# Mamba-2 block and ternary FFN on one core: the scan of sequence 0 issued beside the input projection of sequence 1, with changed start-up order

## Chip, cores and metric

One Trainium2 chip, one of its cores. The metric is the device time of one execution in microseconds; the number that is compared is the median of several executions.

## What is computed

Sixteen sequences of 512 tokens, 256 features each. Float32 throughout, apart from the ternary matmul passes. Cut to what matters, for one x:

```python
x1 = layernorm(x)
zxbcdt = x1 @ in_proj_w.T                    # 256 -> 512 (z) + 768 (xBC) + 8 (dt)
xBC = silu(causal_conv4(xBC) + conv_b)       # -> xs (512), B (128), C (128)
dt = softplus(dt + dt_bias); dA = exp(dt * -exp(A_log))
# for every token, 8 heads of 64 channels, state of 128:
S = dA * S + (xs * dt) outer B;   y = S @ C + D * xs
y = y * silu(z);  y = y * rsqrt(mean(y*y) + 1e-5) * norm_w
x = x + layernorm(x1 + y @ out_proj_w.T)
h = gelu(layernorm(x) @ ternary(W1).T + b1)
x = x + layernorm(h @ ternary(W2).T + b2)
# ternary(w): round(w / mean(|w|)) clipped to -1, 0, 1
```

## The kernel before, in words

The kernel keeps all weights in SBUF and works through the 16 sequences. The order of instructions on PE, ACT, DVE and POOL is written out by hand: every stage is a Python generator that issues instructions and yields a weight of work, and `interleave` (L812) takes, again and again, the next step of the stream that is least far through its window. A stream is given as (generator, work, from, to), with the window as shares of the whole. `run` issues one stage without anything beside it. SP's queue, which carries nearly all DMAs, follows the order of issue.

The stages of one sequence:

- `stage_a0` (L417): statistics of the layernorm on DVE (`bn_stats`, L254), its power on POOL (L261), and four ACT instructions that normalise x to x1 (L285).
- `stage_t0` (L429): PE transposes x1 in eight pieces (L303), ACT copies the two halves to x1T (L306).
- `stage_a` (L312): the input projection in blocks, in the order of a string. "b" is one of six blocks of xBC: four matmuls pm (L325), ACT scales them to cv (L330), DVE adds three convolution taps (L332), and ACT's silu (L339) is held back in a list `late` until the next block. "z" is one of four blocks of z with its silu (L347, L351). "d" makes the rows of dt (L359, L364), "t" turns them over by a PE transpose (L369) and starts the softplus on DVE (L370 to L377). The six blocks and the four of z take PSUM tiles from one pool of four buffers, `ps_a`, which the scan uses too.
- `stage_a1` (L407): the silu that the softplus needs. `stage_a2` (L437): the softplus in 16 small DVE instructions (L444 to L462), then the sums of dt*A over tokens by three kinds of small matmuls (L474, L475), with copies on DVE (L477 to L486) and ACT (L480), and three DMAs that carry the split sums through HBM into the operands lhs_e and rhs_e of the decay matmuls (L488 to L492).
- `stage_b0` and `stage_d` (L499, L514): exponentials of the sums on ACT (L504, L509), written to HBM and broadcast to all partitions as ct (1.5 MB, L519). `stage_e` (L525): POOL multiplies ct by C in three instructions (L530).
- `stage_b1` (L537): for each of four chunks of 128 tokens two decay matmuls pe (L546) and their exponentials mt on ACT (L550).
- `stage_b2` (L555): the scan over the four chunks. `prepare` transposes the inputs (px, L590), makes xdt (L592), the products of B and C (pg, L596 to L603), xend on POOL (L605) and the masked mt (L608) on DVE. Then come pst (L625), the state (L628, L630, L633), the outputs py (L641, L648), y on DVE (L654), the gate zs on POOL (L658), and squares (L569 to L571).
- `stage_c1` and `stage_c2` (L672, L745): output projection, the second layernorm and the feed-forward part, one sequence behind.

Constants for the decay matmuls are made on POOL and ACT by `exponent_constants` (L122). `scales` (L208) folds norm_w into w_out on ACT (L210) and finds the mean of |W| of both ternary weights: a DVE reduction (L215), a matmul with ones (L218), three small DVE instructions (L220 to L223), four POOL comparisons (L227). `ternary` (L231) then makes the ternary weights on DVE.

The start of the kernel, up to sequence 2, is in this order: stage_a of sequence 0 with the constants and the layernorm of sequence 1; stage_a of sequence 1 with stage_a2 of sequence 0 and `scales`; then the scan of sequence 0 with stage_a2 of sequence 1, `ternary(1)` and the layernorm of sequence 2. From sequence 1 on, the scan of a sequence stands beside the feed-forward part of the one before it.

Of the kernel before, what the change touches and what calls it, by code (L numbers as in the profile page):

```python
# [29 lines left out]
F32 = mybir.dt.float32  # L30
# [27 lines left out]
def mamba_ffn_kernel(  # L58
# [96 lines left out]
    nc.scalar.dma_start(cw_sb, conv_w)  # L155
    cb_sb = const.tile([P, NCV], F32)
    nc.scalar.dma_start(cb_sb, conv_b)
    nc.sync.dma_start(win_sb[:, :, 0:DI], win_v[:, :, 0:DI])
    wdt_sb = const.tile([P, 2, 32], F32)
    nc.gpsimd.memset(wdt_sb, 0.0)  # L160
    nc.sync.dma_start(wdt_sb[:, :, 0:NH], win_v[:, :, DI + CONV :])

    dtb = const.tile([P, 1], F32)
    nc.gpsimd.memset(dtb, 0.0)
    for b in range(1, min(3, NB)):
        load_x(b)
# [22 lines left out]
    w1_bf = const.tile([P, 2, FF], BF16)  # L189
    w2_sb = const.tile([P, NF, DM], F32)  # L190
    nc.sync.dma_start(w2_sb, w2.rearrange("(k p) n -> p k n", p=P))
    for c in range(NC):
        nc.sync.dma_start(dtb[32 * c : 32 * c + NH, :], dt_bias.rearrange("(h o) -> h o", o=1))

    negA = const.tile([P, NH], F32)
    nc.scalar.activation(negA, alog, AF.Exp)
# [11 lines left out]
    def scales():  # L208
        for k in range(DI // P):
            nc.scalar.activation(  # L210
                wo_sb[:, k, :], wo_sb[:, k, :], AF.Copy, scale=nw_sb[:, k : k + 1]
            )
        for n, (w, low, _) in ternaries.items():
            part = small.tile([P, 1], F32, tag="tpart", name=f"tpart_{n}")
            nc.vector.tensor_reduce(part, w, AX.XY, ALU.add, apply_absolute_value=True)  # L215
            yield 2.0
            tot = ps_tr.tile([P, 512], F32, tag="tr", name=f"ttot_{n}")
            nc.tensor.matmul(tot[:, 0:1], ones, part, start=True, stop=True)  # L218
# [5 lines left out]
            flat = w.rearrange("p k n -> p (k n)")  # L224
# [84 lines left out]
        return t.rearrange("p (h d) -> p h d", h=NH)  # L309


    def stage_a(b, kinds):  # L312
        x1, x1T = normed.pop(b)


# [6 lines left out]
        def block(m):  # L322
            pm = ps_a.tile([P, L], F32, tag="a", name=f"pm_{b}_{m}")
            for k in range(2):
                nc.tensor.matmul(  # L325
                    pm, win_sb[:, k, DI + m * P : DI + (m + 1) * P], x1T[:, k, :],
                    start=(k == 0), stop=(k == 1),
                )
            cv = sb.tile([P, L], F32, tag="cv", name=f"cv_{b}_{m}", bufs=3)
            nc.scalar.activation(cv, pm, AF.Copy, scale=cw_sb[:, m, 3:4])  # L330
            for j in range(1, 4):
                nc.vector.scalar_tensor_tensor(  # L332
                    cv[:, j:], pm[:, 0 : L - j], cw_sb[:, m, 3 - j : 4 - j], cv[:, j:],
                    ALU.mult, ALU.add,
                )
# [17 lines left out]
        def dt_rows():  # L353


            pq = ps_a.tile([P, L], F32, tag="a", name=f"pq_{b}")
            for k in range(2):
                for c in range(NC):
                    nc.tensor.matmul(  # L359
                        pq[32 * c : 32 * (c + 1), 0:P], wdt_sb[:, k, :],  # L360
                        x1T[:, k, c * P : (c + 1) * P], start=(k == 0), stop=(k == 1),
                    )
            rows = small.tile([P, P], F32, tag="dtr", name=f"dtr_{b}", bufs=1)
            nc.scalar.activation(rows, pq[:, 0:P], AF.Identity, bias=dtb)  # L364
            return rows

        def dt_turned(rows):
            pq = ps_a.tile([P, L], F32, tag="a", name=f"pqt_{b}")
            nc.tensor.transpose(pq[:, 0:P], rows, ident)  # L369
            nc.vector.tensor_copy(  # L370
                dt, pq[:, 0:P].rearrange("p (c h) -> p c h", c=NC)[:, :, 0:NH]
            )

            neg = small.tile([P, NC * NH], F32, tag="sp_n", name=f"sp_n_{b}")
# [31 lines left out]

    def stage_a1(b):  # L407

        s = seqs[b]
        while s["late"]:  # L410
            s["late"].pop()()
        s["sil"] = small.tile([P, NC * NH], F32, tag="sp_s", name=f"sp_s_{b}")
        nc.scalar.activation(s["sil"], s["neg"], AF.Silu)
        yield 0.1

# [51 lines left out]
    def sums_of(b, a):  # L467
# [8 lines left out]
        sums = small.tile([P, 2, W], F32, tag="sums", name=f"sums_{b}")  # L476
        nc.vector.tensor_copy(sums.rearrange("p i w -> p (i w)"), pd[:, 0 : 2 * W])  # L477
        pc = pd[0:W, 2 * W : 2 * W + P]
        cum = small.tile([W, P], F32, tag="dtr", name=f"cum_{b}", bufs=1)
        nc.scalar.copy(cum, pc)  # L480
        cp = small.tile([W, 3, P], BF16, tag="cp", name=f"cp_{b}", bufs=1)
        rest = small.tile([W, P], F32, tag="cr", name=f"cr_{b}", bufs=1)
# [72 lines left out]
    def stage_b2(b):  # L555
        s = seqs[b]
        dt, xbc, zs, dec, mts = s["dt"], s["xbc"], s["zs"], s["dec"], s["mts"]
        ct = s.pop("ct")

        def over_d(t):  # L560
            return t.unsqueeze(2).to_broadcast([P, NH, HD])
# [246 lines left out]
    def chain(*stages):  # L808
        for st in stages:
            yield from st  # L810
# [35 lines left out]
    def run(stage):  # L846
        for _ in stage:
            pass

    with tc.manual_schedule(engines=ordered):  # L850
# [17 lines left out]
        run(stage_a1(1))  # L868
        run(stage_b0(0))
        run(stage_d(0))  # L870
        for i in range(NB - 1):
            if i > 0:
                interleave(
                    (ending(), 0.1, 0.0, 0.01),
                    *([(ternary(2), 4.0, 0.1, 0.7)] if i == 1 else []),
                    *([(stage_a6(i), 0.1, 0.02, 0.03)] if i > 1 else []),
                    (stage_a(i + 1, BESIDE), A_WORK - 1.72, 0.0, 1.0),
                    (stage_c1(i - 1), C1_WORK, 0.0, 1.0),
                    (stage_e(i), E_WORK, 0.06, 1.0),
                )  # L880
                run(stage_a1(i + 1))
# [6 lines left out]
            if i > 0:  # L888
                second.append((stage_c2(i - 1), C2_WORK, 0.02, 1.0))
                second.append((stage_b2(i), B2_WORK, 0.0, 0.98))  # L890
                second.append((stage_a2(i + 1), A2_WORK, 0.15, 0.5))
                second.append((stage_a5(i + 1), 1.7, 0.58, 0.66))
            else:
                second.append((stage_b1(0, 0, NC), 4 * B1_WORK, 0.0, 0.1))
                second.append((stage_e(0), E_WORK, 0.0, 0.3))
                second.append((stage_b2(0), B2_WORK, 0.04, 0.98))
                second.append((stage_a2(1), A2_WORK, 0.03, 0.5))
                second.append((ternary(1), 4.0, 0.3, 0.7))
# [58 lines left out]
```

## Time and profile before

| what | value |
|---|---|
| median of 3 executions | 1191.05 us (1191.03 to 1191.07) |
| profiled execution, its own time | 1192.11 us |
| its span | 1190.4 us |
| busy: PE, DVE, POOL, ACT | 93%, 72%, 50%, 47% |
| PE busy from 0 to 122.73 us | 78.40 us, granted clock 0.83 |
| DVE, ACT, POOL busy from 0 to 122.73 us | 73.04, 49.60, 45.64 us |

The span is what the profile covers; the execution's time lies 1.7 us above it. PE is the matmul engine, PEld its weight loads, DVE, ACT and POOL are VectorE, ScalarE and GpSimd; a `q` behind a name is that engine's DMA issuing. The granted clock is the share of full speed that TensorE had. A name such as pm or xdt is the tile that an instruction writes, and L325 is a line of the kernel. An instruction that waits holds up everything behind it on its own engine.

### The profile page before, as it was taken

To read this page: it belongs to the slowest core of one execution; us is meant where nothing else is said; L and a number is where in the kernel's file an instruction comes from. 1 tells how busy PE (TensorE), PEld (TensorE's weight loads), DVE (VectorE), ACT (ScalarE), POOL (GpSimd) and SP (SyncE) were. 2 spreads that over 40 slices of the span, in tenths; PEclk is the share of its full clock that TensorE was granted. 3 is DMA by queue.
4 is the path that set the end of the run, shared out by engine and by line. 5 is a ranking of instruction groups with operands and counts; after the bars stand their busy time and mean duration, and the time that the engine had idled before them with its cause. 6 is when DMAs were issued, how large, how long until landed. Compare 5 with 4: busy or idle time off the path is not lost.

```text
span 1190.4 us, 16908 instructions
## 1 busy us (share of the span) xinstructions
PE 1112.2 (93%) x6104; PEld 731.1 (61%) x6164; DVE 851.5 (72%) x2213; ACT 564.1 (47%) x951; POOL 595.6 (50%) x707
## 2 busy tenths in 40 slices
PE   6746989999999999999999999999999999998697
PEld 2324557575766757576665757566575757666475
DVE  4766786868777686868768686877768687775552
ACT  4531554645454464546356454635546463542321
POOL 2156545545454555546355454635455454545732
PEclk9877999999999999999999999999999999999899
DMA  5010101010110102011020201002020101101000
GB/s 191 2 55 10 65 4 72 18 66 27 36 57 4 71 19 75 19 57 36 4 74 17 73 19 66 27 4 89 4 71 19 66 27 32 44 4 71 2 9 26
DMA packets 28547, 48.57 MB, mean 41 GB/s; under 512 B 6576, under 2 KB 25648, under 8 KB 26416
## 3 DMA queue, kind: packets, MB, share of 16 engines
q1 hardware_dynamic: 27056, 47.33, 11.7%
q8 instruction: 48, 0.79, 0.3%
q10 hardware_dynamic: 1408, 0.16, 0.1%
q14 instruction: 35, 0.29, 0.1%
HBM read 38.44 MB, written 9.04 MB: 40 GB/s over the span
## 4 chain that ended last, share of the span: by engine, by line
PE 83%; POOL 7%; DVE 6%; ACT 3%; issue 1%; DMA 0%; POOLq 0%; ACTq 0%; DVEq 0%
PE pf L787 19%; PE pm L325 14%; PE ph L753 11%; PE po L707 9%; PE pz L347 8%; PE py L641 5%; PE pst L625 4%; PE py L648 3%; POOL x3p L741 3%; PE pe L546 2%; DVE cv L332 2%; POOL xend L605 1%; PE pt_a L303 1%; PE px L590 1%; PE pss L577 1%; PE pt_f L733 1%
## 5 line engine op out<-in xcount | busy, mean ns | idle before, releaser
L332 DVE SCALAR_TENSOR_TENSOR cv<-pm,cw_sb,cv 128x511 f32<-128x511 f32 (+2 forms) x288 | 215.3, 748 | 54.1 <-ACT cv L330 46.2
L787 PE MATMUL pf<-w_sb,hT 128*128 128x256 f32 x1024 | 248.8, 383 | 0.0
L787 PEld LDWEIGHTS pf<-w_sb,hT 128*128 128x128 f32 x1024 | 189.9, 190 | 42.3 <-issue 14.3
L325 PE MATMUL pm<-x1T,win_sb 128*128 128x512 f32 x384 | 187.9, 614 | 5.1 <-ACT x1T L306 5.1
L753 PE MATMUL ph<-x3p,w_bf 128*128 128x512 bf16 x723 | 181.0, 379 | 6.3 <-ACT x3p L740 1.8
L658 POOL TENSOR_TENSOR zs<-y,zs 128x512 f32<-128x512 f32 x64 | 82.4, 1288 | 203.6 <-DVE y L654 203.6
L759 ACT ACTIVATE hT<-ph,b_sb 128x512 f32<-128x512 f32 x128 | 87.9, 688 | 127.9 <-PE ph L753 91.4
L753 PEld LDWEIGHTS <-w_bf 128*128 128x128 bf16 x768 | 72.7, 98 | 93.3 <-issue 28.3
L550 ACT ACTIVATE mt<-pe 128x512 f32<-128x512 f32 x128 | 74.1, 597 | 116.2 <-PE pe L546 114.1
L707 PE MATMUL po<-wo_sb,zs 128*128 128x256 f32 x512 | 124.3, 387 | 0.3 <-DVE att L713 0.3
L330 ACT ACTIVATE cv<-pm,cw_sb 128x512 f32<-128x512 f32 x96 | 65.7, 684 | 123.8 <-PE pm L325 122.2
L347 PE MATMUL pz<-x1T,win_sb 128*128 128x512 f32 x256 | 121.9, 599 | 0.0
L325 PEld LDWEIGHTS pm<-x1T,win_sb 128*128 128x128 f32 x384 | 72.5, 196 | 78.8 <-issue 67.7
L530 POOL TENSOR_TENSOR ct<-ct,xbc 128x1024 f32<-128x1024 f32 x48 | 113.4, 2375 | 12.5 <-DVE sp_a L456 12.5
L707 PEld LDWEIGHTS po<-wo_sb,zs 128*128 128x128 f32 x512 | 95.7, 192 | 28.5 <-issue 17.1
L654 DVE SCALAR_TENSOR_TENSOR y<-xbc,dsk,py 128x128 f32<-128x128 f32 x256 | 71.2, 340 | 44.0 <-PE py L648 23.5
L641 PE MATMUL py<-mt,xdt 128*64 128x128 f32 x1024 | 99.2, 289 | 2.7 <-DVE y L654 2.3
L793 DVE TENSOR_TENSOR o<-pf,b_sb 128x256 f32<-128x256 f32 x64 | 26.9, 420 | 88.1 <-PE pf L787 88.1
L641 PEld LDWEIGHTS py<-mt,xdt 128*64 128x64 f32 x1024 | 62.9, 143 | 32.9 <-issue 18.6
L347 PEld LDWEIGHTS pz<-x1T,win_sb 128*128 128x128 f32 x256 | 47.9, 193 | 56.1 <-issue 48.2
L351 ACT ACTIVATE zs<-pz 128x512 f32<-128x512 f32 x64 | 37.9, 592 | 87.5 <-PE pz L347 87.3
L648 PE MATMUL py<-ct,state 128*64 128x128 f32 x768 | 78.2, 283 | 0.0
(137 smaller groups left out, 1805.3 us busy)
## 6 DMA issues: line engine op xcount, KB each, us to landing
ct<-way SPq DMA_DIRECT2D x16, 1536.0 KB
xin<-in_x SPq DMA_DIRECT2D x16, 512.0 KB
out<-o SPq DMA_DIRECT2D x30, 256.0 KB
w_in<-in_w SPq DMA_DIRECT2D x1, 1024.0 KB
w_sb<-in_w SPq DMA_DIRECT2D x1, 1024.0 KB, 11.0
win_sb<-in_w_in SPq DMA_DIRECT2D x1, 768.0 KB
win_sb<-in_w_in SPq DMA_DIRECT2D x1, 512.0 KB
wo_sb<-in_w_out SPq DMA_DIRECT2D x1, 512.0 KB
```

Of the source, the lines that this page charges most:

```text
L325: nc.tensor.matmul(pm, win_sb[:, k, DI + m * P : DI + (m + 1) * P], x1T[:, k, :], start=(k == 0), stop=(k == 1),)
L332: nc.vector.scalar_tensor_tensor(cv[:, j:], pm[:, 0 : L - j], cw_sb[:, m, 3 - j : 4 - j], cv[:, j:], ALU.mult, ALU.add,)
L347: nc.tensor.matmul(pz, win_sb[:, k, j * P : (j + 1) * P], x1T[:, k, :], start=(k == 0), stop=(k == 1),)
L530: nc.gpsimd.tensor_tensor(ct[:, c - 1], ct[:, c - 1], xbc[:, 5, c * P : (c + 1) * P].unsqueeze(1).to_broadcast([P, NH, P]), ALU.mult,)
L550: nc.scalar.activation(mt[:, hs, :].rearrange("p h t -> p (h t)"), pe, AF.Exp)
L641: nc.tensor.matmul(py[h % 2 * HD : (h % 2 + 1) * HD, j, :], xdt[:, h * HD : (h + 1) * HD], mts[c][:, h, :], start=True, stop=(c == 0),)
L648: nc.tensor.matmul(py[h % 2 * HD : (h % 2 + 1) * HD, j, :], state[:, h * HD : (h + 1) * HD], ct[:, c - 1, h, :], start=False, stop=True,)
L658: nc.gpsimd.tensor_tensor(zs[:, :, tok], y, zs[:, :, tok], ALU.mult)
L707: nc.tensor.matmul(po[:, 0:DM], g[:, k, c * P : (c + 1) * P], wo_sb[:, k, :], start=(k == 0), stop=(k == NJ - 1),)
L753: nc.tensor.matmul(ph, w1_bf[:, k, f * P : (f + 1) * P], x3p[:, j, k, :], start=(j == 0 and k == 0), stop=(j == 2 and k == 1),)
L759: nc.scalar.activation(hT[:, f, :], ph, AF.Gelu, bias=b1_sb[:, f : f + 1])
L787: nc.tensor.matmul(pf[:, 0:DM], hT[:, f, c * P : (c + 1) * P], w2_sb[:, f, :], start=(f == 0), stop=(f == NF - 1),)
```

## The change

Ten small edits, all in the start-up. The input of sequence 1 is loaded ahead of z's weights. dt_bias is broadcast over partitions by one DMA on ACT's queue, in place of four on SP's, and is added by DVE after the transpose of dt, in place of ACT before it. The sums of |W| are made by ACT (Abs with an accumulator) in place of DVE. `stage_a` gets a lag for its held silus, two blocks for sequence 0. `stage_sil` is split from `stage_a1`. The tile `cum` gets a buffer of its own. The strings of blocks for sequences 0 and 1 put dt second. The statistics of sequence 1 are issued ahead of sequence 0's convolutions, and softplus and sums of sequence 0, and `scales`, in its `stage_a`. The scan of sequence 0 is interleaved with `stage_a` of sequence 1, together with its own softplus, the decay matmuls of sequence 1, the layernorm of sequence 2 and `ternary(1)`. In POOL's order xend of chunks 0 and 1 comes ahead of the first product on ct.

```diff
-    nc.sync.dma_start(win_sb[:, :, 0:DI], win_v[:, :, 0:DI])
     wdt_sb = const.tile([P, 2, 32], F32)
     nc.gpsimd.memset(wdt_sb, 0.0)
     nc.sync.dma_start(wdt_sb[:, :, 0:NH], win_v[:, :, DI + CONV :])
-
-    dtb = const.tile([P, 1], F32)
-    nc.gpsimd.memset(dtb, 0.0)
-    for b in range(1, min(3, NB)):
-        load_x(b)
+    load_x(1)
+    nc.sync.dma_start(win_sb[:, :, 0:DI], win_v[:, :, 0:DI])
+    load_x(2)
+    dtb = const.tile([P, NH], F32)
+    nc.scalar.dma_start(dtb, dt_bias.partition_broadcast(P))
...
-    for c in range(NC):
-        nc.sync.dma_start(dtb[32 * c : 32 * c + NH, :], dt_bias.rearrange("(h o) -> h o", o=1))
...
-            nc.vector.tensor_reduce(part, w, AX.XY, ALU.add, apply_absolute_value=True)
+            flat = w.rearrange("p k n -> p (k n)")
+            nc.scalar.activation(low, flat, AF.Abs, accum_out=part)
...
-    def stage_a(b, kinds):
+    def stage_a(b, kinds, lag=1):
...
-            while late:
-                late.pop()()
             late.append(
...
+            if len(late) > lag:
+                late.pop(0)()
...
-            nc.scalar.activation(rows, pq[:, 0:P], AF.Identity, bias=dtb)
+            nc.scalar.copy(rows, pq[:, 0:P])
...
-            nc.vector.tensor_copy(
-                dt, pq[:, 0:P].rearrange("p (c h) -> p c h", c=NC)[:, :, 0:NH]
-            )
+            nc.vector.tensor_tensor(
+                dt, pq[:, 0:P].rearrange("p (c h) -> p c h", c=NC)[:, :, 0:NH],
+                dtb.unsqueeze(1).to_broadcast([P, NC, NH]), ALU.add,
+            )
...
     def stage_a1(b):
 
+        late = seqs[b]["late"]
+        while late:
+            late.pop()()
+        yield from stage_sil(b)
+
+    def stage_sil(b):
...
-        cum = small.tile([W, P], F32, tag="dtr", name=f"cum_{b}", bufs=1)
+        cum = small.tile([W, P], F32, tag="cum", name=f"cum_{b}", bufs=1)
...
-    EVEN, BESIDE = "bzbdzbtzbzbb", "bbdtzbzbzbz"
+    FIRST, SECOND, BESIDE = "bdbtbzbzbzbz", "bdbtzbzbzbzb", "bbdtzbzbzbz"
...
         interleave(
             (
-                chain(stage_a0(0), stage_t0(0), stage_a(0, EVEN)),
+                chain(stage_a0(0), stage_t0(0), stage_a(0, FIRST, 2)),
                 A0_WORK + T0_WORK + A_WORK, 0.0, 1.0,
             ),
-            (exponent_constants(), 9.0, 0.15, 0.9),
-            (stage_a0(1), A0_WORK, 0.4, 0.9),
+            (exponent_constants(), 9.0, 0.1, 0.5),
+            (stage_a0(1), A0_WORK, 0.04, 0.28),
+            (chain(stage_sil(0), stage_a2(0)), 0.1 + A2_WORK, 0.42, 0.85),
+            (scales(), 6.0, 0.55, 1.0),
         )
         run(stage_t0(1))
-        run(stage_a1(0))
+        run(stage_a6(0))
         interleave(
-            (stage_a2(0), A2_WORK, 0.0, 0.6),
-            (scales(), 6.0, 0.35, 0.9),
-            (stage_a(1, EVEN), A_WORK, 0.0, 1.0),
+            (stage_a(1, SECOND), A_WORK, 0.0, 0.8),
+            (stage_b0(0), 0.1, 0.11, 0.111),
+            (stage_d(0), 0.1, 0.111, 0.112),
+            (stage_b1(0, 0, NC), 4 * B1_WORK, 0.112, 0.1121),
+            (stage_b2(0), B2_WORK, 0.2, 0.9),
+            (stage_e(0), E_WORK, 0.3, 0.65),
+            (chain(stage_sil(1), stage_a2(1)), 0.1 + A2_WORK, 0.3, 0.75),
+            (stage_a0(2), A0_WORK, 0.6, 0.85),
+            (ternary(1), 4.0, 0.75, 0.95),
+            (stage_a6(1), 0.1, 0.86, 0.861),
+            (stage_b0(1), 0.1, 0.88, 0.881),
+            (stage_b1(1, 0, 2), 2 * B1_WORK, 0.89, 0.9),
+            (stage_b1(1, 2, 4), 2 * B1_WORK, 0.94, 0.98),
+            (stage_d(1), 0.1, 0.95, 0.96),
+            (stage_t0(2), T0_WORK, 0.96, 1.0),
         )
-        run(stage_a1(1))
-        run(stage_b0(0))
-        run(stage_d(0))
-        for i in range(NB - 1):
-            if i > 0:
+        for i in range(1, NB - 1):
...
             second.append((stage_c2(i - 1), C2_WORK, 0.02, 1.0))
             second.append((stage_b2(i), B2_WORK, 0.0, 0.98))
...
```

More of the change, by code (lines that the diff above doesn't have):

```diff
@@ L223, in scales @@
             nc.vector.tensor_scalar_mul(nhalf, half, -1.0)
-            flat = w.rearrange("p k n -> p (k n)")
             for j in range(4):
@@ L369, in dt_turned @@
             nc.tensor.transpose(pq[:, 0:P], rows, ident)
-            nc.vector.tensor_copy(
-                dt, pq[:, 0:P].rearrange("p (c h) -> p c h", c=NC)[:, :, 0:NH]
+            nc.vector.tensor_tensor(
+                dt, pq[:, 0:P].rearrange("p (c h) -> p c h", c=NC)[:, :, 0:NH],
+                dtb.unsqueeze(1).to_broadcast([P, NC, NH]), ALU.add,
             )
-            neg = small.tile([P, NC * NH], F32, tag="sp_n", name=f"sp_n_{b}")
+            neg = small.tile([P, NC * NH], F32, tag="sp_n", name=f"sp_n_{b}", bufs=2)
             df = dt.rearrange("p c h -> p (c h)")
@@ L407, in stage_a1 @@
     def stage_a1(b):
+        late = seqs[b]["late"]
[3 more added lines that the diff above has]
+    def stage_sil(b):
         s = seqs[b]
-        while s["late"]:
-            s["late"].pop()()
-        s["sil"] = small.tile([P, NC * NH], F32, tag="sp_s", name=f"sp_s_{b}")
+        s["sil"] = small.tile([P, NC * NH], F32, tag="sp_s", name=f"sp_s_{b}", bufs=1)
         nc.scalar.activation(s["sil"], s["neg"], AF.Silu)
@@ L557, in stage_b2 @@
         dt, xbc, zs, dec, mts = s["dt"], s["xbc"], s["zs"], s["dec"], s["mts"]
-        ct = s.pop("ct")
+        ct = s["ct"]
         def over_d(t):
@@ L860, in mamba_ffn_kernel @@
+            (scales(), 6.0, 0.55, 1.0),
         )
         run(stage_t0(1))
-        run(stage_a1(0))
+        run(stage_a6(0))
         interleave(
-            (stage_a2(0), A2_WORK, 0.0, 0.6),
-            (scales(), 6.0, 0.35, 0.9),
-            (stage_a(1, EVEN), A_WORK, 0.0, 1.0),
-        )
-        run(stage_a1(1))
-        run(stage_b0(0))
-        run(stage_d(0))
-        for i in range(NB - 1):
-            if i > 0:
[L873 to L879, printed above, removed]
-                )
-                run(stage_a1(i + 1))
+            (stage_a(1, SECOND), A_WORK, 0.0, 0.8),
[13 more added lines that the diff above has]
+            (stage_t0(2), T0_WORK, 0.96, 1.0),
+        )
@@ L882, in mamba_ffn_kernel @@
+        for i in range(1, NB - 1):
+            interleave(
+                (ending(), 0.1, 0.0, 0.01),
+                *([(ternary(2), 4.0, 0.1, 0.7)] if i == 1 else []),
+                *([(stage_a6(i), 0.1, 0.02, 0.03)] if i > 1 else []),
+                (stage_a(i + 1, BESIDE), A_WORK - 1.72, 0.0, 1.0),
+                (stage_c1(i - 1), C1_WORK, 0.0, 1.0),
+                (stage_e(i), E_WORK, 0.06, 1.0),
+            )
+            run(stage_a1(i + 1))
             second = [
@@ L887, in mamba_ffn_kernel @@
             ]
[L888 to L898, printed above, removed]
+            second.append((stage_c2(i - 1), C2_WORK, 0.02, 1.0))
+            second.append((stage_b2(i), B2_WORK, 0.0, 0.98))
+            second.append((stage_a2(i + 1), A2_WORK, 0.15, 0.5))
+            second.append((stage_a5(i + 1), 1.7, 0.58, 0.66))
             second.append((stage_d(i + 1), 0.1, 0.92, 0.93))
```

## Prediction

> **What bounds the kernel now.** I read the page first: PE is busy 93% of the span, so the steady part has little to give, and its slices fall only at the two ends. Then busy time by stretch, cut where the first convolution matmul of sequences 1 (39.20) and 2 (122.73) starts. Columns: length, then busy time of PE, PEld, DVE, ACT, POOL, granted clock, DMA share, GB/s.
>
> ```profile
> 39.20:122.73 83.53, 54.42 (x248) 30.29 (x250) 54.62 (x120) 28.67 (x57) 35.65 (x28) 0.76 0.12 40
> 122.73:190.00 67.27, 63.36 (x354) 40.55 (x357) 54.21 (x132) 31.50 (x54) 32.80 (x37) 1.00 0.08 24
> 190.00:257.00 67.00, 66.25 (x376) 43.52 (x379) 51.52 (x136) 33.57 (x57) 35.11 (x42) 1.00 0.10 33
> ```
>
> From 192.95 on a sequence takes 68.5 us (x1T copies at 192.95, 261.45, 329.95; the first such step, from 121.40, takes 71.55), and PE is busy 66.25 of 67.00 at clock 1.00. There the kernel is bound by PE and the change leaves its work and order alone. Ahead of that PE idles 83.53 - 54.42 = 29.1 us, and at clock 0.76 about 0.24 x 54.4 = 13.1 us of its busy time is clock: 42 us in one stretch. No engine there exceeds 65%; it is bound by waits. So the forecast is one difference: when does sequence 2's first matmul start, 122.73 now. What it gains goes through one to one, because PE has no slack behind it.
>
> The waits of the first 122.7 us (total, times, longest):
>
> ```profile
> DVE cv L332 <- ACT cv L330: 21.4, 8, 9.1
> ...
> ACT cum L480 <- DVE sums L477: 11.1, 2, 8.6
> ...
> PE pst L625 <- DVE sp_a L456: 6.7, 1, 6.7
> ...
> PE pm L325 <- ACT x1T L306: 5.1, 1, 5.1
> PE ttot L218 <- DVE tpart L215: 4.9, 1, 4.9
> ...
> PE pe L546 <- DMA rhs_e<-away: 3.9, 1, 3.9
> ```
>
> DVE waits for convolutions while PE waits for the scan's inputs, one after the other: the scan of sequence 0 has no matmul-rich neighbour. Last, rows in order of time (start, duration) that price operations:
>
> ```profile
> 46.86 0.87 DVE L456 SCALAR_TENSOR_TENSOR sp_a<-sp_a,sp_e 128x32 f32<-128x32 f32 x4
> ...
> 50.95 2.28 DVE L215 TENSOR_REDUCE tpart<-w_in 128x1 f32<-128x2048 f32 x1
> ...
> 73.26 0.21 ACT L413 ACTIVATE sp_s<-sp_n 128x32 f32<-128x32 f32 x1
> 73.49 1.28 ACT L504 ACT_TABLE_LOAD   x1
> ...
> 74.78 0.26 ACT L504 ACTIVATE dec<-sums 128x64 f32<-128x64 f32 x1
> ...
> 82.64 3.82 DVE L456 SCALAR_TENSOR_TENSOR sp_a<-sp_a,sp_e 128x32 f32<-128x32 f32 x4
> 83.07 2.34 POOL L530 TENSOR_TENSOR ct<-ct,xbc 128x1024 f32<-128x1024 f32 x1 [12.52 <-DVE sp_a L456]
> ```
>
> The same four DVE instructions take 0.87 alone and 3.82 beside POOL's ct product. Convolution taps (one operand from PSUM) keep their 0.75 beside POOL.
>
> **Part 1, up to sequence 1's first matmul (39.20 now).** The start to 16.5 stays: pm of block 0 ends there at half clock. Moved onto the SP queue ahead of z's weights is load_x(1). SP's third issue waits for a small ACT-queue load until 7.55, as now, so x_1 takes the slot of z's weights; the 4 MB behind move at 340 to 400 GB/s from 11 on, so x_1 lands near 12.5, z's weights near 14 (needed at 21), wdt near 16. wdt is needed at 16.5 instead of 20.3; I charge nothing, up to 1.5 if it is late. The dt_bias broadcast is one more ACT-queue DMA and replaces four tiny SP issues (4.7 us of SP, after which dt_rows waited 2.2 now); DVE adds the bias in the instruction that copied: 0.2 either way.
>
> Sequence 1's statistics take DVE 4 x 0.53 + 0.35 = 2.5 us, 12.5 to 15, ahead of the first taps, which can't start before 17.3: covered. The queue behind it on DVE is all taps; cover gone means 1:1. POOL's power and product (1.2) follow, and all rhs_e/lhs_e constants (6.3) now stand behind them, done near 22.7 instead of 31.6; ACT's copies want them at 24: covered. ACT puts the four x_1 (2.07) ahead of cv 1, so cv 1 comes at 20.5 instead of near 19: 1 us on DVE.
>
> Following the ACT and DVE orders with row durations (cv 0.69, silu 0.71, zs 0.59, rhs_e copy 1.03, taps 2.32): cv 2 ends 21.8, table load 23.1, silu, copies and softplus silu to 27.7, cv 3 28.4, silu, w_out scaling 1.69, absolute sum, zs 1, cv 4 at 34.0. PE, done with pm 4 at 28, stands at ttot for the absolute sum until 32.7: 4.8 us idle, half clock behind it. DVE does taps 3 to 30.7, twelve softplus steps (0.19 each) to 33.0, taps 4 to 36.3, thalf, sums. ACT's cum, behind silu 2, waits for these sums to 37.0 (2.3; the same row has 2.5 now), then zs 2, absolute sum, cv 5 at 40.7; taps 5 end at 43.0, thalf 43.5. PE's transposes of x_1 stand behind the second ttot and share its two PSUM buffers, so they wait for that thalf; with the x1T copies, sequence 1's matmul starts near 45.4. That is 6.2 later, with sequence 0's softplus, sums and both scales already done.
>
> Absolute sums: DVE loses 2 x 2.28. On ACT no such row exists; two of the 1024-wide copies give 2 x 1.03, less one fixed part: 1.9 to 2.1. The Trainium skill ("ScalarE: Activation LUTs", Rules for kernel authors) says simple arithmetic belongs on VectorE, per element up to about three times faster. By that rule 2.28 on DVE would become some 6.8; by the rows 1.9. I take the rows: the DVE price is a measured float32 reduction, and the rule's factor is for bf16. The accumulator may add 0 to 0.3 each.
>
> **Part 2, to sequence 2's first matmul (83.5 now).** PE does pm 0, pq, pm 1 by 50.3 (first at half clock); ACT cv 0, dt, cv 1, silu 0, then the exp table at 51.7, dec, cum, eight mt (0.5 each) from 53.6 to 57.7. Their inputs by DMA: cp at 38.5, landing 4 us later, so the 3.9 wait for rhs_e goes. The pe matmuls take turns through PSUM with mt; pqt, queued behind them, comes at 56.5, and DVE, whose next instruction it feeds, idles 53.3 to 56.6. What is late next is this: 3.3 us that did not exist.
>
> Chunk 0 prepares on DVE 59.0 to 61.5 (xdt 0.69, two small 0.6, mt 1.21), chunk 1 to 64.0. xend now stands ahead of ct on POOL: today xend of chunk 0, ready at 80.2, ran at 85.4 behind ct, which waited for its 1.5 MB broadcast; pst now runs at 62.0. The broadcast, issued 55.2, needs 6.4 (76.7 to 83.1 now): 61.6, no wait. Then DVE is the chain: taps 2 to 66.3, y0 1.1, four softplus steps, chunk 2 2.5, four steps, state, taps 3 to 76.6, y1 to 77.7, eight steps, chunk 3 2.5, taps 4, state to 87.5, half the statistics, sums, y2 to 91.4, rest, taps 5 from 92.9 to 95.2. Pure DVE work from 48.7 to 95.2 is 36.3 (taps 13.9, chunks 9.4, y 3.4, softplus and dt 4.1, states 1.4, statistics 2.8, sums 1.3); 3.3 is the pqt idle; the rest, 6.9, is short waits and contention.
>
> Contention is the unknown. Sixteen softplus steps fall beside POOL's ct, zs, state. Ends: 0 if none collides; 16 x 2.1 = 34 if each waits as the worst row (L462: 2.27 for 0.19). I take 5.5, near today's 2.95 + 0.97 + 2.08 = 6.0 of the same steps of sequence 1. PE waits for a at 82: 4.4 idle, half clock for a few us, hidden by DVE.
>
> The tail: silu 5 at 96.4 (behind the four x_2), exp table 98.4, dec, cum 98.9, seven mt 102.4, x1T; matmul of sequence 2 near 103.5. w_bf (2.6) hides beside mt. I add 2.5 for some 25 handovers at 0.1 that I rounded away: **106**.
>
> Tables: the exp/silu alternation adds two loads. The skill (same page, Table sets: the hidden batching unit) says to do all of one set before switching, and prices a switch at about 2.66 with its drain: 5.3. The rows show silu ending 73.47, load 1.28, exp at 74.78: no drain seen, 2.6. One more lies on my chain than now; it is in the walk at 1.28. By the rule it would be 1.4 later.
>
> Sum: 122.73 - 106 = 16.7, rounded to 16. The profiled execution took 1192.11 with span 1190.4 and gives 1176.1 and 1174.4; the median of 3, 1191.05, is 1.06 below it, so **1175.0**.
>
> **Rivals.** (a) Waits vanish more than I think: DVE from 48.7 with 36.3 of work and no idle ends at 85, tail 8.3, so 93 to 96 and a gain of 27 to 29: 1163. For it: PE gets matmul cover, clock 1.00. Against: pqt and POOL. Chance 0.10.
>
> (b) The early statistics and absolute sums stretch part 1: wdt late 1.5, cold clock, ttot; 8 us more than walked: 1183. Chance 0.20.
>
> (c) Slower: the second softplus now runs amid POOL's scan products. At 2.1 for each of 16 steps, 34 instead of 5.5 on the DVE chain, sequence 2 starts at 134.5, 12 later: 1203. It decides from 5.5 + 16.7 = 22 us of contention on (1.4 a step). For it the row 3.82; against it, ten of the sixteen steps today kept 0.2. Chance 0.09.
>
> (d) The new order shifts waits only, within 2.4 us: 1191. Chance 0.03. My forecast: 0.58.
>
> A measurement can tell about 0.2%, 2.4 us, from no change. Range 1166 to 1188: the forecast +-9 and most of (b); left out are (a), (c), (d). Faster 0.88, same 0.03, slower 0.09.
>
> **What would show it.** After: the first matmul of sequence 2 near 106, sequence 1 near 45; clock in between above 0.9; no pst wait behind ct; two more ACT_TABLE_LOAD at 1.28; ACTIVATE of 128x2048 near 1.9; DVE's wait at dt for pqt near 3; 71.6 and then 68.5 us per sequence behind. Wrong if the softplus steps of sequence 1 together exceed 12 us, if x_1's statistics hold the first taps, or if the steady stretch changes.

## The result and the profile after

The changed kernel takes 1174.79 us in the median of 4 runs (1172.91 to 1177.73), the kernel before 1191.04 on the same chip (4 runs, 1190.73 to 1191.07): ratio 0.9869, 95% interval 0.9855 to 0.9883. The forecast was 1175.0. The profiled execution took 1172.91 us with a span of 1171.1, which is 19.2 us less than the profiled execution of before. Line numbers from here on are those of the changed kernel: pm is L323, cv L328, the taps L330, the softplus L447 to L465, the sums pd L477, ct L533, pe L549, mt L553, px L593, xdt L595, xend L608.

Sequence 1's first matmul starts at 42.05 us (39.20 before) and sequence 2's at 102.90 (122.73 before). The busy times by stretch, cut at these two points, in the same columns as before (length; PE, PEld, DVE, ACT, POOL; granted clock, DMA share, GB/s):

```profile
42.05:102.90 60.85, 45.43 (x241) 24.51 (x240) 47.12 (x94) 29.53 (x54) 29.30 (x25) 0.82 0.11 37
102.90:170.00 67.10, 64.06 (x351) 40.83 (x351) 53.54 (x129) 30.55 (x52) 31.76 (x36) 0.96 0.10 34
170.00:237.00 67.00, 66.46 (x380) 43.52 (x379) 51.86 (x137) 33.72 (x57) 34.13 (x42) 1.00 0.10 33
```

The stretch is 60.85 us in place of 83.53, and it starts 2.85 later: 22.68 - 2.85 = 19.8 us are won at the start of sequence 2. Behind it the x1T copies come at 102.15, 173.96, 242.45 and 310.95: one step of 71.8 and then 68.5, against 71.55 and 68.5 before. So 0.3 us of the 19.8 is given back in the first step, and nearly all of the rest arrives at the end (the span is 19.3 shorter). The stretch is denser but not full: PE idles 60.85 - 45.43 = 15.4 us (29.1 before), and its clock is 0.82.

The waits of the first 103 us (total, times, longest) show what took the place of the old ones:

```profile
ACT cum L483 <- DVE sums L480: 14.9, 2, 12.5
...
PE pd L477 <- DVE a L465: 8.4, 2, 8.1
DVE cv L330 <- ACT cv L328: 8.2, 7, 2.9
...
PE ttot L216 <- ACT w_in L213: 3.9, 1, 3.9
DVE xdt L595 <- PE px L593: 3.9, 1, 3.9
```

DVE's wait for convolutions falls from 21.4 to 8.2. PE's waits for pst (6.7) and pm (5.1) are gone, and the one for rhs_e falls from 3.9 to 1.6. In their place PE waits 8.1 us for the softplus of sequence 1 (row "PE pd"), and DVE waits for pqt, PE's transpose of dt (3.0), and then for px (3.9). In order of time:

```profile
52.62 0.19 DVE L368 TENSOR_TENSOR dt<-pqt,dtb 128x32 f32<-128x32 f32 x1 [2.98 <-PE pqt L367]
52.86 3.77 PE L345 MATMUL pz<-x1T,win_sb 128*128 128x512 f32 x4 [0.28 <-DVE dt L368]
57.11 0.69 DVE L595 TENSOR_TENSOR xdt<-px,dt 128x512 f32<-128x512 f32 x1 [3.86 <-PE px L593]
```

ACT's rows of the same execution, in order of time, price the two operations on which the prediction weighed a rule:

```profile
29.61 1.90 ACT L213 ACTIVATE w_in<-w_in 128x2048 f32<-128x2048 f32 x1
31.41 0.19 ACT L213 ACTIVATION_READ_ACCUMULATOR w_in<-w_in 128x1 f32 x1
...
96.45 0.70 ACT L335 ACTIVATE xbc<-cv,cb_sb 128x512 f32<-128x512 f32 x1
97.16 1.28 ACT L507 ACT_TABLE_LOAD   x1
98.45 0.26 ACT L507 ACTIVATE dec<-sums 128x64 f32<-128x64 f32 x1
```

The absolute sum is 1.90 plus a separate instruction of 0.19 that reads the accumulator. The table switch is 1.28, with the last silu ending 0.01 ahead of it and dec starting 0.01 behind: no drain.

### The profile page after: what moved, and what is told of

It reads as the page before. It is cut to its first block, busy times and chain, and to the rows that moved or that the text cites. A ratio compares the mean times of both kernels' runs of the same rounds, so it can differ in the third digit from the quotient of the medians.

```text
span 1171.1 us, 16958 instructions
## 1 busy us (share of the span) xinstructions
PE 1110.8 (95%) x6164; PEld 727.9 (62%) x6164; DVE 849.0 (72%) x2211; ACT 568.0 (48%) x957; POOL 593.7 (51%) x706
## 4 chain that ended last, share of the span: by engine, by line
PE 83%; DVE 6%; POOL 6%; ACT 3%; DMA 1%; issue 1%; POOLq 0%; ACTq 0%; DVEq 0%
PE pf L790 20%; PE pm L323 12%; PE ph L756 12%; PE po L710 9%; PE pz L345 8%; PE py L644 5%; PE pst L628 4%; PE py L651 3%; POOL x3p L744 3%; PE pe L549 2%; DVE cv L330 1%; POOL xend L608 1%; PE pt_a L300 1%; PE px L593 1%; PE pt_f L736 1%
## 5 line engine op out<-in xcount | busy, mean ns | idle before, releaser
L330 DVE SCALAR_TENSOR_TENSOR cv<-pm,cw_sb,cv 128x511 f32<-128x511 f32 (+2 forms) x288 | 215.3, 747 | 44.8 <-ACT cv L328 36.9
L756 PE MATMUL ph<-x3p,w_bf 128*128 128x512 bf16 x768 | 189.0, 381 | 4.2 <-ACT x3p L743 1.7
L323 PE MATMUL pm<-x1T,win_sb 128*128 128x512 f32 x384 | 184.1, 602 | 0.0
L756 PEld LDWEIGHTS <-w_bf 128*128 128x128 bf16 x768 | 72.9, 98 | 93.8 <-issue 29.1
L553 ACT ACTIVATE mt<-pe 128x512 f32<-128x512 f32 x128 | 73.6, 595 | 110.3 <-PE pe L549 110.3
L328 ACT ACTIVATE cv<-pm,cw_sb 128x512 f32<-128x512 f32 x96 | 65.7, 684 | 118.7 <-PE pm L323 117.1
L323 PEld LDWEIGHTS pm<-x1T,win_sb 128*128 128x128 f32 x384 | 70.9, 193 | 71.8 <-issue 65.7
L533 POOL TENSOR_TENSOR ct<-ct,xbc 128x1024 f32<-128x1024 f32 x48 | 113.3, 2374 | 0.0
L611 DVE SCALAR_TENSOR_TENSOR mt<-mt,pg 128x1024 f32<-128x1024 f32 x64 | 77.6, 1212 | 0.5
```

The source lines that it names most:

```text
L323: nc.tensor.matmul(pm, win_sb[:, k, DI + m * P : DI + (m + 1) * P], x1T[:, k, :], start=(k == 0), stop=(k == 1),)
L330: nc.vector.scalar_tensor_tensor(cv[:, j:], pm[:, 0 : L - j], cw_sb[:, m, 3 - j : 4 - j], cv[:, j:], ALU.mult, ALU.add,)
L533: nc.gpsimd.tensor_tensor(ct[:, c - 1], ct[:, c - 1], xbc[:, 5, c * P : (c + 1) * P].unsqueeze(1).to_broadcast([P, NH, P]), ALU.mult,)
L553: nc.scalar.activation(mt[:, hs, :].rearrange("p h t -> p (h t)"), pe, AF.Exp)
L611: nc.vector.scalar_tensor_tensor(mts[c], mts[c], 1.0, cbt.unsqueeze(1).to_broadcast([P, NH, P]), ALU.min, ALU.mult)
L756: nc.tensor.matmul(ph, w1_bf[:, k, f * P : (f + 1) * P], x3p[:, j, k, :], start=(j == 0 and k == 0), stop=(j == 2 and k == 1),)
```

## Experiments

My theory (A): the overlap of scan and blocks (part 2) brings most of the gain, and what the new stretch still pays is DVE's small softplus steps beside POOL's products. Rivals: the gain is mostly part 1's (B), or the stretch is bound by PE's order or ACT's. Each run below has a median of its own runs, and a ratio to the kernel before, which ran beside it on the same chip.

**The changed kernel again, without an edit (again).**

> The changed kernel once more, unaltered, since its four times lie 4.8 us apart where those of before lie 0.3 apart. If the spread is TensorE's clock in the start-up (it comes and goes with idle gaps), another execution has the same instruction durations on DVE, ACT and POOL, and its first matmul of sequence 2 moves by up to 5 us with a lower granted clock ahead of it. If it is DMA landing times, the waits that move are those on lhs_e, rhs_e or ct. Expected median 1172 to 1178.

1176.68 us (1175.95 to 1177.89, 4 runs), 0.9876 [0.9864, 0.9889]. Sequence 1 starts at 44.88 here and sequence 2 at 105.86, both 2.8 to 3 us later than in the first profile; the stretch between is 61.0 against 60.85. The difference lies ahead of 42 us: x_1's statistics start at 13.89 in place of 12.91, and PE stands at pq for the dt weights, here for 1.90 us and before for 0.28:

```profile
17.47 0.64 PE L357 MATMUL pq<-x1T,wdt_sb 128*32 128x128 f32 x16 [1.90 <-DMA wdt_sb<-in_w_in]
```

The delay grows on its way: 1.1 us at pq, 2.2 at the second block's taps (22.06 in place of 19.90), 2.8 at sequence 1. Here the growth begins at the four pm matmuls behind the longer wait, which run at a lower clock (3.26 us at a granted 0.59, in place of 1.98 at 1.00). Where it falls differs: in the run no_ct0 below pq is as late (17.48) and these four take 1.98, but the last block's pm take 2.85 in place of 1.88, and sequence 1 starts at 44.85 all the same. So two executions of one kernel differ by 3 us, beginning with the landing of loads; how the first 1.1 us becomes 2.8 is not settled. In what follows the stretches are compared, not only their ends.

**Part 2 undone (scan_apart).** The blocks of sequence 1 run first and the scan of sequence 0 behind them, in the order of before; part 1 stays.

```diff
+        run(stage_a(1, SECOND))
+        run(stage_a1(1))
+        run(stage_b0(0))
+        run(stage_d(0))
         interleave(
-            (stage_a(1, SECOND), A_WORK, 0.0, 0.8),
...
+            (stage_b1(0, 0, NC), 4 * B1_WORK, 0.0, 0.1),
+            (stage_e(0), E_WORK, 0.0, 0.3),
+            (stage_b2(0), B2_WORK, 0.04, 0.98),
+            (stage_a2(1), A2_WORK, 0.03, 0.5),
...
```

> The second part undone: sequence 1's blocks are issued first, then the scan of sequence 0 in the order of before, with all of part 1 kept. Theory A, the overlap of the scan with the blocks brings most of the gain: 1186 to 1189. Theory B, from the rows: the blocks alone take about 17 us from 42 on, the scan then the 50 us that it took before (72.5 to 122.7), so sequence 2 starts near 110 and the time is 1180 to 1183; part 1, which takes softplus and scales out from between the blocks, then brings more than half.

1185.27 us (1183.67 to 1186.27, 5 runs), 0.9946 [0.9935, 0.9958]: 6.5 us faster than before, 8.6 slower than the whole change. It misses theory A's interval by 0.7 us and theory B's by 2.3. Its two stretches, blocks and scan:

```profile
46.00:67.00 21.00, 18.89 (x62) 7.93 (x60) 13.63 (x22) 11.55 (x19) 6.17 (x4) 1.00 0.00 1
67.00:117.44 50.44, 27.09 (x179) 17.62 (x180) 31.74 (x69) 16.05 (x33) 23.26 (x20) 0.76 0.17 64
```

The scan alone takes 50.4 us with PE busy for 27.1 of them; before it took 50.1 (72.60 to 122.73). The blocks alone take 21.0 at full clock, since the softplus, the sums and the scales of sequence 0 are done by then; before, with these among them, 33.4. Apart they add up to 71.4, together they take 61: the overlap saves 10.5 us in the stretch.

**Part 1's order undone, part 2 kept (part2_alone).** Blocks, constants, statistics, softplus and scales of the first two sequences go back to the old order; the loads, dt_bias and the absolute sums on ACT stay changed.

```diff
-                chain(stage_a0(0), stage_t0(0), stage_a(0, FIRST, 2)),
+                chain(stage_a0(0), stage_t0(0), stage_a(0, "bzbdzbtzbzbb")),
...
-            (exponent_constants(), 9.0, 0.1, 0.5),
-            (stage_a0(1), A0_WORK, 0.04, 0.28),
-            (chain(stage_sil(0), stage_a2(0)), 0.1 + A2_WORK, 0.42, 0.85),
-            (scales(), 6.0, 0.55, 1.0),
+            (exponent_constants(), 9.0, 0.15, 0.9),
+            (stage_a0(1), A0_WORK, 0.4, 0.9),
...
+            (stage_a2(0), A2_WORK, 0.0, 0.1),
+            (scales(), 6.0, 0.05, 0.5),
```

> The issue order of part 1 undone, part 2 kept: sequence 0's softplus, its sums and the scales are issued at the head of the second stretch, block strings of sequence 0, statistics of sequence 1 and constants as before; the load order, the bias on DVE and the absolute sums on ACT stay. Theory A: 1176 to 1179, near the full change. Theory B: the scan can't start until the softplus of sequence 0 is through, about 8 to 10 us into the stretch, so sequence 2 starts near 110 and the time is 1180 to 1184.

1181.7 us (1179.38 to 1183.3, 6 runs), 0.9919 [0.9906, 0.9932]. Sequence 1 starts at 37.91, 4 to 7 us earlier than with the whole change, and sequence 2 at 112.05, 6 to 9 later: what part 1 does ahead of sequence 1 costs up to 7 us there and saves 13 in the stretch (74.1 against 61). Part 2 alone wins 10.1 us and part 1 alone 6.5; the sum, 16.6, is about the whole (15.1 in the same comparison). Both kernels keep the new loads, the dt_bias broadcast and the sums on ACT, so what these are worth is counted twice in that sum: seen from the whole change, undoing part 2 costs 8.6 us and undoing part 1's order 5.0. Neither part needs the other. Part 2 is about three fifths of the gain either way: most of it, but theory A, which expected 1176 to 1179 here, made part 1 too small.

**POOL's three ct products of sequence 0 left out (no_ct0).**

```diff
-            (stage_e(0), E_WORK, 0.3, 0.65),
```

> The changed kernel without POOL's three products on ct for sequence 0 (the multiplication of the broadcast decays by C is left out, so sequence 0 is computed without it). If the sixteen softplus steps of sequence 1 are stretched by POOL's use of SBUF, they fall from 11.9 us in sum to 5 to 7, and the time falls by 4 to 6 us, to 1169 to 1171. If they only fill time in which DVE would wait for something else, the steps get shorter and the time stays within 1.5 us.

1170.06 us (1169.27 to 1170.55, 4 runs), 0.9819 [0.9806, 0.9832]: 6.6 us below the changed kernel beside it. Between the two profiled executions (1170.55 and 1175.95) the difference is 5.4, and 4.9 of it lies in the stretch (44.85 to 100.92, 56.1 against 61.0). The sixteen softplus steps of sequence 1 sum to 6.6 in place of 11.9, 5.3 less, and nearly all of this is what the stretch wins. Their last steps here:

```profile
79.82 0.19 DVE L461 SCALAR_TENSOR_TENSOR sp_a<-sp_a,sp_z 128x32 f32<-128x32 f32 x1
79.92 0.17 DVE L462 TENSOR_SCALAR dt<-dt 128x32 f32<-128x32 f32 x1
80.14 0.66 DVE L463 SCALAR_TENSOR_TENSOR dt<-sp_a,dt 128x32 f32<-128x32 f32 x1
```

and in the changed kernel, DVE and POOL in order of time:

```profile
74.49 4.46 DVE L459 SCALAR_TENSOR_TENSOR sp_a<-sp_a,sp_e 128x32 f32<-128x32 f32 x4
75.88 2.34 POOL L533 TENSOR_TENSOR ct<-ct,xbc 128x1024 f32<-128x1024 f32 x1
...
79.39 1.04 POOL L633 TENSOR_TENSOR state<-state,dec 128x512 f32<-128x512 f32 x1
79.40 1.06 DVE L462 TENSOR_SCALAR dt<-dt 128x32 f32<-128x32 f32 x1
80.39 2.34 POOL L533 TENSOR_TENSOR ct<-ct,xbc 128x1024 f32<-128x1024 f32 x1
80.50 2.27 DVE L463 SCALAR_TENSOR_TENSOR dt<-sp_a,dt 128x32 f32<-128x32 f32 x1
```

L462 ends 0.03 us behind POOL's state (79.40 + 1.06 against 79.39 + 1.04), L463 0.04 behind POOL's ct. A small step is not slowed by a factor: it stands until POOL's instruction is over. L459's four fall from 4.46 to 1.93 without ct. PE's wait for a falls from 8.1 to 2.8 with it.

**Absolute sums back on VectorE (sum_dve).**

```diff
-            nc.scalar.activation(low, flat, AF.Abs, accum_out=part)
+            nc.vector.tensor_reduce(part, w, AX.XY, ALU.add, apply_absolute_value=True)
```

> The changed kernel with the two absolute sums back on VectorE (a reduction of 128x2048, 2.28 us each in the trace of before, against 1.90 + 0.19 measured on ScalarE). Theory of the rows: ScalarE stands at cum for VectorE's sums in this stretch (2.3 us) while VectorE is full of taps, so the reduction delays the sums and everything behind by about 2 us at each of two places, of which about half shows: 1177 to 1179, 0.5 to 2.5 above the changed kernel on the same chip (1176.7). Rival, the rule that simple arithmetic belongs on VectorE: TensorE's wait at ttot (3.9) ends earlier, ScalarE is relieved by 4.2 us and the kernel is 1 to 3 us faster.

1178.58 us (1176.71 to 1180.99, 5 runs), 0.9896 [0.9877, 0.9915], against 0.9876 of the changed kernel: 1.9 us slower in the medians, with intervals that overlap. The trace speaks more clearly than the time: PE's wait at ttot does not end earlier, it grows from 4.1 (in the repeat of the changed kernel) to 5.3, since the reduction stands behind taps on DVE, and ACT's wait at cum grows from 2.3 to 5.8.

```profile
PE ttot L216 <- DVE tpart L213: 5.3, 1, 5.3
```

Sequence 1 starts at 48.07 against 44.88, of which up to 0.6 is later landing of x_1. A gain of 1 to 3 us from the rule is excluded by the two intervals; how much ScalarE is worth, between nothing and some 5 us, is not settled by the time.

**Statistics of sequence 1 back behind the convolutions (stats_late).**

```diff
-            (stage_a0(1), A0_WORK, 0.04, 0.28),
+            (stage_a0(1), A0_WORK, 0.4, 0.9),
```

> The changed kernel with the statistics of sequence 1 put back behind the first three convolutions on VectorE (and the four normalising instructions on ScalarE as far back). In the changed kernel they run from 12.9 to 15.9, before the first convolution can start, and cost VectorE nothing there. If that cover is worth what they take (2.5 us of VectorE, and 2.07 us of ScalarE), VectorE's queue up to sequence 1 is 2 to 3 us longer: 1178 to 1180. Rival: ScalarE, not VectorE, sets the pace up to there, and taking the x_1 wait off VectorE's queue and four instructions off ScalarE's early queue brings the first convolutions forward: 1 to 2 us faster, 1174 to 1176. TensorE's waits for the absolute sums decide it if neither moves the start of sequence 1 (42 to 45).

1178.11 us (1175.8 to 1179.13, 5 runs), 0.9883 [0.9865, 0.99]; sequence 1 starts at 44.92 (44.88 in the repeat of the changed kernel), sequence 2 at 105.77. The statistics stand among the taps now (at 25.65 and 30.76), the first taps start at 16.49 (16.33 in the repeat), and sequence 1 starts where it did. The median lies just inside the interval of the first theory (1178 to 1180), but the longer queue that it names is not there, and the interval overlaps that of the changed kernel: the early statistics are worth nothing that these runs can tell, up to some 3 us.

**ct ahead of xend again (ct_ahead).**

```diff
-            (stage_e(0), E_WORK, 0.3, 0.65),
+            (stage_e(0), E_WORK, 0.199, 0.65),
```

> The changed kernel with one thing undone in GpSimd's order: the first product on ct stands ahead of xend of chunks 0 and 1 again, as before the change. In the trace of the changed kernel xend of chunk 0 runs at 57.95 and ct only at 61.15, when its broadcast has landed; with ct ahead, xend waits to 63.5, pst comes near 64.4 in place of 59.73, y of chunk 0 near 66.4 in place of 63.87. If the order of xend was worth what VectorE then waits: 2 to 3 us slower than the changed kernel (1178 to 1180, first matmul of sequence 2 near 105 to 108). Rival: VectorE is so full that y of chunk 0 is hidden, or the softplus steps behind it only meet less of GpSimd's work: no difference within 1 us.

1176.92 us (1176.0 to 1177.32, 4 runs), 0.9877 [0.986, 0.9894]: no difference. The stretch is 61.05 (45.95 to 107.00). POOL's rows show the new order:

```profile
61.31 2.36 POOL L533 TENSOR_TENSOR ct<-ct,xbc 128x1024 f32<-128x1024 f32 x1 [8.90 <-ACT zs L349]
63.63 2.04 POOL L608 TENSOR_TENSOR xend<-xdt,dec 128x512 f32<-128x512 f32 x2
```

pst starts at 64.72, 3.3 us behind the xdt of chunk 0, in place of 2.6. DVE is in taps 2 meanwhile (65.97 to 68.28) and goes on to y without a wait. The broadcast has landed by 61.31, just as the xdt of chunk 0 begins (61.44), so xend waits 2.3 us at most, and DVE's taps cover them. My expectation took a wait on POOL for one on DVE.

**The dt weights loaded ahead of x_1 (wdt_first).**

```diff
+    wdt_sb = const.tile([P, 2, 32], F32)
+    nc.gpsimd.memset(wdt_sb[:, :, NH:], 0.0)
     nc.sync.dma_start(win_sb[:, :, DI:], win_v[:, :, DI : DI + CONV])
+    nc.sync.dma_start(wdt_sb[:, :, 0:NH], win_v[:, :, DI + CONV :])
...
-    wdt_sb = const.tile([P, 2, 32], F32)
-    nc.gpsimd.memset(wdt_sb, 0.0)
-    nc.sync.dma_start(wdt_sb[:, :, 0:NH], win_v[:, :, DI + CONV :])
```

> The changed kernel with the small load of the dt weights issued ahead of x_1 on SyncE's queue (only its padding is set by GpSimd, so the load waits for nothing). If the spread of the changed kernel (first matmul of sequence 2 at 102.9 in one execution, 105.9 in another, with the same instruction times) comes from when these loads land: pq no longer waits for the dt weights (0.3 and 1.9 in those two), 1173 to 1175, and a range under 1.5 us. Rival: x_1 and z's weights land later by what the small load takes of the queue, about as much is lost as won: 1176 to 1178, with the same spread.

1173.68 us (1171.5 to 1174.28, 4 runs), 0.9851 [0.9834, 0.9867]. The median is where the theory put it, and pq no longer waits for its weights (it runs at 16.00), but x_1's statistics start at 14.06 and the range is 2.8 us, not under 1.5. The two intervals touch: a gain of about 3 us is likely, not shown, and the spread has more than this one cause.

**Softplus of sequence 1 where DVE idled (plus_early).** The sixteen steps go up behind taps 1, ahead of POOL's first product; their silu runs ahead of the exp table's load. In the string of sequence 1 the transpose of dt ("t") also moves ahead of the second block. `first(n, stage)` issues the next n steps of a stage.

```diff
-    FIRST, SECOND, BESIDE = "bdbtbzbzbzbz", "bdbtzbzbzbzb", "bbdtzbzbzbz"
+    FIRST, SECOND, BESIDE = "bdbtbzbzbzbz", "bdtbzbzbzbzb", "bbdtzbzbzbz"
...
+            (first(1, plus := chain(stage_sil(1), stage_a2(1))), 0.1, 0.121, 0.122),
...
+            (first(4, plus), 0.7, 0.126, 0.127),
...
-            (chain(stage_sil(1), stage_a2(1)), 0.1 + A2_WORK, 0.3, 0.75),
+            (plus, 0.3, 0.21, 0.22),
```

> The changed kernel with the sixteen softplus steps of sequence 1 moved up to right behind taps 1 of sequence 1, where VectorE stands idle for pqt and GpSimd has not begun its ct product; their table is the silu table that is loaded there anyway, so one pair of table loads goes as well. If the contention beside GpSimd (11.9 us of steps against about 3.4 alone) and the wait for pqt are what the stretch still pays: the steps sum to below 4 us, TensorE's wait for a of 8.1 goes, and sequence 2 starts 9 to 11 us earlier: 1166 to 1168. Rival: the moved steps push the preparation of chunk 0 and with it TensorE's first scan product back by as much as they take, and other waits come in their place: 1171 to 1174.

1166.45 us (1165.86 to 1167.82, 4 runs), 0.9795 [0.9779, 0.981], as the theory had it. The stretch is 51.96 (44.48 to 96.44) in place of 61, and the same instructions take

```profile
53.84 0.65 DVE L456 SCALAR_TENSOR_TENSOR sp_a<-sp_a,sp_e 128x32 f32<-128x32 f32 x3
54.52 0.87 DVE L459 SCALAR_TENSOR_TENSOR sp_a<-sp_a,sp_e 128x32 f32<-128x32 f32 x4
```

against 1.56 and 4.46. All sixteen sum to 3.4 us in place of 11.9. The clock of the stretch is 0.91. The 9 us are not contention alone: pqt comes before DVE asks for it (47.41), so the 3.0 us wait is gone, and the steps fill time in which DVE waited for px (2.19 of 3.86 is left). New waits take part of it back, 2.35 and 1.63 us for POOL's state. The pair of table loads that was to go stays (50.98 and 56.56).

**In addition the layernorm of sequence 2 ahead of the exp table (plus_t0_early).**

```diff
-            (stage_t0(2), T0_WORK, 0.96, 1.0),
+            (stage_t0(2), T0_WORK, 0.862, 0.87),
```

> As the kernel with the softplus steps moved up, and in addition the transposes of x_2 and their copies ahead of the exp table and the mt products of sequence 1 at the end of the stretch. In the changed kernel the last x1T copy (102.15) stands behind eight mt activations of 0.5 us. If the order on ScalarE there is on the chain, a further 2 to 4 us: 1163 to 1165. Rival: the mt products are then late for TensorE's scan of sequence 1, and what is gained at the start of sequence 2 is given back within it: no difference to the kernel without this edit (within 1 us).

1167.55 us (1164.87 to 1168.42, 5 runs), 0.9799 [0.9781, 0.9817]: no difference, as the rival said, but not for its reason. x1T is ready at 92.96, and yet pm waits until 97.16, because PE's own queue has the pe matmuls ahead of it, and these wait for mt to free PSUM:

```profile
95.25 2.02 PE L549 MATMUL pe<-rhs_e,lhs_e 128*128 128x512 bf16 x4 [0.25 <-ACT mt L553]
97.16 2.41 PE L323 MATMUL pm<-x1T,win_sb 128*128 128x512 f32 x3
```

**Both gains together (both).** The softplus moved up and the dt weights first.

> The kernel with the softplus steps of sequence 1 moved up (1166.45 measured) together with the dt weights loaded ahead of x_1 (3.0 us below the changed kernel in median, measured). They act in different stretches, before 42 us and after it, so they should add: 1163 to 1165, with a range under 2 us. If the second gain was only the spread of the landing times, the sum stays at 1165 to 1167.

1164.25 us (1163.33 to 1165.52, 5 runs), 0.9774 [0.9755, 0.9792]: the fastest kernel here, about 12 us below the changed one. It starts sequence 1 at 40.66 and sequence 2 at 93.61. Its interval overlaps that of the softplus move alone, so that move is what is shown; the range, 2.2 us, is a little over what I expected.

## Why the prediction was right, and where it was not

The time, the sign and the mechanism came out: 1175.0 against 1174.79, and the mechanism, the scan's gaps filled by matmuls of sequence 1, is what the runs with each part alone show. That the two figures agree to 0.2 us is luck: the four times lie between 1172.91 and 1177.73, the repeat gave 1176.68, and in the first profile sequence 2 starts 3.1 us ahead of the forecast of 106 (102.90; 105.86 in the repeat). Step by step:

- **Start of sequence 1, forecast 45.4: measured 42.05 and 44.88.** pq at 16.5 (16.35), the wait at ttot 4.8 (3.9), ACT's wait at cum 2.3 (2.34) and the absolute sum 1.9 to 2.1 plus 0 to 0.3 (1.90 + 0.19) were right. One step failed: "they wait for that thalf", for PE's transposes of x_1. They ran at 40.2 and 41.55, the second waiting 0.68 for the first x1T copy only, while the second ttot's tnhalf came only at 42.56. That step was about 2 us too late in the forecast (an estimate: its 45.4 counts from thalf at 43.5, while the absolute sum that the transposes do wait for ends there near 40). "Up to 1.5 if it is late", for the dt weights, came true in the repeat with 1.9; that its 44.88 is near 45.4 comes from this, not from the step. x_1's statistics, a sign of being wrong if they held the first taps, ended at 15.42 ahead of taps at 16.84; where x_1 landed later they did hold them, by 0.3 to 0.7 us in five runs (in the run both cv ends at 15.76 and the taps start at 16.47), without loss, since the taps of the second block waited 1.9 to 3.8 us for their own cv anyway.
- **The stretch, forecast 60.6: measured 60.85 and 61.0.** Its total hides two terms that were too small. Contention was taken as 5.5; the sixteen steps took 11.9 where 3.4 is their time alone, 8.5. Behind pqt (3.3 forecast, 2.98 measured) a second wait was not seen: pz, at a granted clock of 0.50 after PE's own wait of 2.18 for cum, took 3.77 for four matmuls in place of 1.98, and xdt waited 3.86 for px behind it. Together 6.9 too little, and 2.9 of it was offset by terms taken too large. The walk from the first taps to the end of taps 5 gave 46.5 and took 50.5 (44.77 to 95.25); the first taps came 0.6 sooner behind the first matmul, the tail took 7.65 for 8.3, and the 2.5 us "for some 25 handovers" covered the rest. So the sum is right because an allowance without a mechanism was about as large as what was missed.
- **Contention, its size.** The price "2.1 for each" step was the wrong unit. The rows above show a step standing until POOL's instruction ends, so the bound is POOL's own busy time beside those steps: between 64.89 and 82.81 POOL is busy 12.5 us, and rival (c)'s 34, or the 22 from which it decides, could not be reached there. The Trainium skill ("SBUF — State Buffer", "SBUF: two separate sides") says the same: the port pair that VectorE and GpSimd share is an exclusive lock, held for a whole instruction, which a VectorE instruction with two SBUF inputs, or in a two-port mode, needs. Read ahead of the prediction it would have given POOL's work as the bound in place of 34. My own threshold for being wrong, over 12 us for all steps, was only just not reached (11.9 here and in the repeat).
- **TensorE's wait for a, forecast 4.4 at 82: measured 8.1 at 83.06.** The contention above. The wait itself was hidden by DVE, as forecast: from 57.11 to 95.25 DVE never waits for PE and idles only 0.32 us. What costs time is the stretched steps on DVE, as no_ct0 shows (steps 5.3 us shorter, stretch 4.9).
- **"No pst wait behind ct": right, but worth nothing.** The wait is gone from the list, and ct_ahead puts xend back without a change in the time.
- **Clock above 0.9: wrong, 0.82.** PE still idles a quarter of the stretch, and matmuls behind its waits run at half clock: 0.50 from 49.70 to 56.50, behind 2.18 us, and from 83.06 to 87.20, behind 8.11. The gain did not need it: idle fell by 13.7 us, clock loss only from 13.1 to about 8 (0.18 x 45.4).
- **Tables and the steady part: right.** Loads at 47.92 and 53.50 are the two more, 1.28 each; the drain that the Trainium skill adds ("ScalarE: Activation LUTs", What ACT_TABLE_LOAD costs, 2.66 us in all) shows in no row here. 71.8 and 68.5 us per sequence.
- **The rivals.** (a), 1163, is nearly what the kernel reaches with the softplus moved out of POOL's way (1166.45, with the dt weights 1164.25): the reason given against it ("pqt and POOL") was the right one. (b) is there in a small form, as the 3 us between executions. (c) and (d) did not come.

## What to carry to other kernels

Two stages that are each bound by waits can share their time when one has the matmuls and the other the gaps: of the 21.0 us of blocks half was hidden here, and with the small steps moved nearly all (51.96 us together, 50.4 for the scan alone). The gain can be predicted as one event's date, walked through the queue of the engine that will be fullest. When small VectorE steps are moved into such an overlap, lay them where GpSimd is idle: their price there is not their length but what is left of GpSimd's instruction. And an allowance in a sum should have a name: where it has none, a right total says little about the steps.

## What the runs showed of the hardware

- VectorE steps of 128x32 with SBUF operands end with the GpSimd instruction that runs beside them (0.19 becomes 2.27 beside a 2.34 us product). The reciprocal, with one input, is an exception: it keeps its 0.35 at 65.11 beside POOL's zs (65.06 to 66.33). xdt and the taps, with an operand in PSUM, keep theirs too: 0.69 for xdt at 61.44 beside ct in ct_ahead, and 2.31 for three taps at 61.64 beside ct in the changed kernel.
- An accumulator on ScalarE costs a second instruction of 0.19 us, and its 1.90 and 0.19 together for 128x2048 float32 are less than VectorE's reduction (2.28).
- Loads land at different times from run to run: in the eight profiled executions here with the same loads ahead of them (the changed kernel twice, scan_apart, no_ct0, sum_dve, ct_ahead and the two kernels with the softplus moved but the old loads), x_1's statistics start between 12.91 and 14.53, and pq between 16.35 and 17.76.
